# A four-layer graph network on one core: a larger dense part in the last layer, its own-weight products made a stage earlier, and wider sharing of overflow chunks

## The chip, the cores and the metric

The kernel runs on one core of a Trainium2 chip. The metric is the time of one execution in device microseconds, as the median over runs. The engines are named as in the profile: PE is TensorE (PEld its weight loads), DVE is VectorE, ACT is ScalarE, POOL is GpSimd, SP is SyncE, which issues most of the plain transfers.

## The reference

There are 6250 nodes with 256 features and 100000 edges (`src`, `dst`), sorted by `dst`. Four layers follow each other, each `x = layernorm(x + layer(x))` without gain:

```python
# layer 0: SAGE on h = relu(layernorm(x) * gamma + beta)
out = mean_over_edges(h[src] -> dst) @ W_l.T + b_l + h @ W_r.T
# layer 1: attention with 8 heads; softmax over the edges of one src
s = <q[src], k[dst]>; out = segment_sum(softmax(s) * v[dst], src) @ Wo + bo
# layer 2: two GAT passes with 4 heads, self loops, gelu; softmax over the edges of one dst
e = leaky_relu(alpha_s[src] + alpha_d[dst], 0.2); out = segment_sum(h[src] * softmax(e), dst) + b
# layer 3: SAGE, relu, a further product, residual, relu
mean = segment_sum(x[src], dst) / max(cnt, 1)
sage = mean @ W_l.T + b_l + x @ W_r.T
out = relu(relu(sage) @ W_ln.T + x)
```

## The kernel before

**Tiling.** The nodes are cut into `NB = 50` blocks of `B = 125`. The edges of a block are laid out in `CM = 16` chunks of 128 edges; what does not fit goes to `SH = 2` shared chunks, which one group of `GB = 10` blocks has in common (`NGR = 5` groups). A chunk's node rows are fetched from a table in HBM by an indirect transfer that POOL issues (`gather`, L927), 128 rows at a time, one instruction for each chunk. The sum over the edges of a block is then a product on PE: a one-hot matrix of the targets (made by DVE, or in layer 1 by PE and ACT) times the fetched rows.

**Stages.** The first stage, with its order of instructions written out by hand, normalises `x` in ten groups of five blocks (`Rows`) and stores them in three bf16 parts to `h_table` (`write`, L1170). Beside it, `by_target` makes the lists of edges by target, one part for each `next(lists)`. Then come five passes over the blocks: layer 0 (`piece0`, table `h_table`, with the lists by source made beside it in `by_source`), layer 1 (`piece1`, tables `kv_table` and `q_table`), the two GAT passes of layer 2 (`piece2`, `hs_tables`), and layer 3 (`piece3`, `x_table`). In layers 1 and 2 a pass has 200 pieces of four chunks.

**Order.** `run_pass` starts one piece after another and, at each start, advances every open piece by one `yield`, the oldest first; then it calls a function for work beside the pass. A scheduler may still move instructions on an engine. Gathers run ahead of their use by as many pieces as the `g` buffers hold: 7 in layer 1, 9 in layer 2, 5 in layer 3. The last step of a block is `finish0` to `finish3`. `finish2` of the second GAT pass updates `x_sb`, normalises it and stores its bf16 parts to `x_table`.

**The dense part of the last layer.** For the first `ND = 16` blocks of targets, layer 3 does not fetch edges. During the GAT passes, `count_edges` counts the edges from each source block to these targets: DVE compares target numbers with the edge ends (`a_hot`, L1897), PE multiplies (`a_acc`, L1919, one PSUM bank), ACT evicts a row group of `RB = 4` target blocks (500 columns) to `a_row` (L1906), and SP stores the row to `a_table` in bf16. Not all chunks can hold edges to a row group: `reach` gives the chunks for each. One step handles up to three chunks of one row group, and one step is made for each piece. In layer 3 `dense` loads rows of `x_table` (`xs`) and counts (`cnt`), 50 pairs of loads, and multiplies them (L2180); `RATE` spreads this over the first 80% of the pieces of the other 34 blocks. `finish3` makes the products with `W_l` and `W_r` (L923), the relu, the product with `W_ln` and the last normalisation.

`move` splits a transfer over more than 112 partitions into 112 and the rest:

```python
if B > HW_SPLIT:
    eng.dma_start(out=to[:HW_SPLIT], in_=of[:HW_SPLIT])
    eng.dma_start(out=to[HW_SPLIT:], in_=of[HW_SPLIT:])
```

Of the kernel before, what the change touches and what calls it, by code (L numbers as in the profile page):

```python
# [8 lines left out]
I32 = mybir.dt.int32  # L9
F16 = mybir.dt.float16  # L10
# [6 lines left out]
P = 128  # L17
# [638 lines left out]
def gnn_stack_kernel(ctx: ExitStack, tc: tile.TileContext, ins, out):  # L656
# [21 lines left out]
    GB = max(n for n in range(1, 11) if NB % n == 0)  # L678
# [33 lines left out]
    ND, RB = 16, 4  # L712
# [10 lines left out]
    DC = max(c1 for c0, c1 in reach)  # L723

# [15 lines left out]
    with ExitStack() as fast:  # L740
# [45 lines left out]
        a_table = dram.tile([N, ND * B], BF16, name="a_table_f")  # L786
# [51 lines left out]
        def block_rows(table, b, n=1):  # L838

            t = table[b * B : (b + n) * B, :]  # L840
            return t if n == 1 else t.rearrange("(n p) d -> p n d", p=B)
# [269 lines left out]
        class Rows:  # L1111
# [57 lines left out]
            def write(self):  # L1169
                nc.sync.dma_start(out=block_rows(h_table, self.b0, self.n), in_=self.hp)  # L1170
# [17 lines left out]
        with tc.tile_pool(name="fst", bufs=1) as pool, tc.tile_pool(name="fh", bufs=2) as work, tc.tile_pool(  # L1188
# [26 lines left out]
            for t in range(len(groups) + 5):  # L1215
                for r in group(t - 4):
                    r.low()
                for r in group(t - 3):
                    r.high()
                for r in group(t - 1):  # L1220
                    r.normal()
                if t == 1:
                    nc.vector.tensor_copy(gamma_p, gamma)
                for r in group(t - 2):
                    r.gain(gamma_p, beta)
                for r in group(t):
                    r.variance()
                if 1 <= t <= 6 or t == len(groups) - 1:
                    next(lists)
                for r in group(t - 3):  # L1230
                    last_h = r.rest()
                for r in group(t - 5):
                    r.write()
# [635 lines left out]
        beside_2 = ExitStack()  # L1869
        ap = beside_2.enter_context(tc.tile_pool(name="fa", bufs=2))  # L1870
        apsum = beside_2.enter_context(tc.tile_pool(name="fap", bufs=1, space=bass.MemoryType.PSUM))

        def count_edges():


            nodes = ap.tile([P, ND, B], F16, name="a_nodes", bufs=1)
            nc.vector.scalar_tensor_tensor(
                nodes, iota[:, :ND, None].to_broadcast([P, ND, B]), float(B),
                iota_p[:, None, :B].to_broadcast([P, ND, B]), op0=ALU.mult, op1=ALU.add,
# [10 lines left out]
            for k in range(len(steps) + 2):  # L1890
                if k < len(steps):
                    s, r, cs = steps[k]
                    if s not in sts:
                        sts[s] = one_hots(ap, key_s[:, s, :DC], DC, DC, 2, F16, "a_st")
                    hots[k] = ap.tile([P, 3, RW], F16, name="a_hot", bufs=3)
                    for i, c in enumerate(cs):
                        nc.vector.tensor_scalar(  # L1897
                            hots[k][:, i, :], nodes[:, r * RW : (r + 1) * RW], ends[:, s, c : c + 1], None,
                            op0=ALU.is_equal,
                        )  # L1900
                if k >= 2:
                    s, r, cs = steps[k - 2]
                    if cs[-1] == reach[r][1] - 1:
                        if r == 0:
                            rows[s] = ap.tile([B, ND * B], BF16, name="a_row")
# [24 lines left out]
        for layer in range(2):  # L1930
            table = hs_tables[layer]
            with tc.tile_pool(name=f"f2{layer}", bufs=1) as pool, tc.tile_pool(
# [4 lines left out]
                bias = load_row(pool, ins[f"L2_gnn_b{layer}"], "bias")  # L1937
                w_gat = gat_weight(pool, work, 1) if layer == 0 else None
                sums, held, shared, late = {}, {}, {}, []

                def finish2(b):
# [17 lines left out]
                    else:  # L1959
# [5 lines left out]
                        move(nc.sync, block_rows(x_table, b), xp.rearrange("p k d -> p (k d)"))  # L1965

# [90 lines left out]
                run_pass([(lambda a=a: piece2(*a)) for a in pieces((4, 4, 4, 4))], lambda t: next(counting, None))  # L2057
# [15 lines left out]
        beside_2.close()  # L2073
# [3 lines left out]
        with tc.tile_pool(name="f3", bufs=1) as pool, tc.tile_pool(name="f3w", bufs=2) as work, tc.tile_pool(  # L2077
# [5 lines left out]
            w_r = load_weight(pool, ins["L3_gnn_W_r"], "w_r")  # L2083
# [7 lines left out]
            def finish3(b, aT=None):  # L2091

                if aT is None:
                    agg = work.tile([B, D], F32, name="agg")
                    nc.scalar.activation(agg, sums.pop(b)[:B], AF.Copy, scale=rdeg[:, b, :])
                    yield
                    sum_T = kept(work, turned(bank(), agg), "aT")
                    yield
                xT = kept(work, turned(bank(), x_sb[:, b, :]), "xT")
# [3 lines left out]
                if aT is None:  # L2103
                    product(po, [(sum_T, w_l), (xT, w_r)])
                    nc.vector.tensor_add(s, po, b_l[:B, :])
                else:
                    product(po, [(aT, w_l)])
                    nc.vector.scalar_tensor_tensor(s, po, rdeg[:, b, :], b_l[:B, :], op0=ALU.mult, op1=ALU.add)
                    yield
                    po = bank()[:B, :D]  # L2110
                    product(po, [(xT, w_r)])
                    nc.vector.tensor_add(s, s, po)
# [44 lines left out]
            def load(k):  # L2157
# [3 lines left out]
                cnt = work.tile([B, 2, GW], BF16, name="cnt", bufs=LEAD + 2)  # L2161
                rows = a_table[s * B : (s + 2) * B, d * GW : (d + 1) * GW]
                move(nc.sync, cnt, rows.rearrange("(n p) d -> p n d", p=B))
                return xs, cnt

            ready = []

            def dense():
                loads = {k: load(k) for k in range(LEAD)}
                for k, (d, s) in enumerate(order):  # L2170
                    if k + LEAD < len(order):
                        loads[k + LEAD] = load(k + LEAD)
                    xs, cnt = loads.pop(k)
# [86 lines left out]
```

## Time and profile before

| | us |
|---|---|
| median of 14 runs (lowest, highest) | 5158.46 (5152.07, 5162.97) |
| the profiled execution: its own time | 5164.1 |
| its span, first to last instruction | 5162.3 |
| busy: PE, DVE, ACT, POOL | 4241.6, 3532.5, 2163.5, 3776.6 |
| start of the first and of the last gather from `h_table` | 149.2 to 1249.3 |
| start of the first and of the last gather from `kv_table` | 1235.4 to 2289.8 |
| start of the first and of the last gather from `hs_tables` | 2333.3 to 4421.4 |
| start of the first and of the last gather from `x_table` | 4443.3 to 5134.3 |

The profile is of one execution. A line of its list of groups has the source line, engine, operation, what is written and read, the count, the busy time and the mean of one in ns, and after the bar the idle time of the engine ahead of these instructions with what ended most of it. "issue" means that the engine waited for nothing that the profile shows. The rows by stage give the busy time of each engine within a stretch of the span. Matmuls are pipelined, so a mean duration of one is longer than what it adds to a row of them.

### The profile page before, as it was taken

The page shows a single profiled execution, that of the slowest core. Times are in us where ns is not written, and L with a number is a line of the kernel's source. Part 1 is how long each engine was busy: PE and PEld are TensorE (multiplying, and loading weights), DVE is VectorE, ACT ScalarE, POOL GpSimd, SP SyncE. Part 2 cuts the span into 40 slices and gives each one's busy share as a digit, 9 for nine tenths or more (in the row PEclk, how much of TensorE's full clock was granted, in tenths as well). Part 3 has the DMA queues.
Part 4 walks back from the last instruction along what each step waited for, and adds up shares of the span by engine and source line. Part 5 has one row for each costly group of instructions (what it writes and reads, how often), then busy time and mean ns, then how long its engine had stood idle before and what let it go on. Part 6 is the DMA issues. An engine that isn't in the chain of part 4 may idle for free. (4 is left out here: it accounts for less than half of the span.)

```text
span 5162.3 us, 84598 instructions
## 1 busy us (share of the span) xinstructions
PE 4241.6 (82%) x27926; PEld 3093.3 (60%) x27926; DVE 3532.5 (68%) x10485; ACT 2163.5 (42%) x6203; POOL 3776.6 (73%) x3889
## 2 busy tenths in 40 slices
PE   0467899987999999987887878877777777799996
PEld 0245667666676666665666666655556566466665
DVE  7576788766888888876666666657777777423334
ACT  4011898895344444433444444434444444211122
POOL 6677777776777777757777777767777777677775
PEclk9777999998999999998989999988989998899998
DMA  4556677666777777764444444444444444788875
GB/s 131 145 155 176 178 193 192 186 175 176 222 226 227 223 227 226 226 177 122 132 132 134 135 131 134 129 117 131 132 132 134 132 138 135 210 244 241 248 206 142
DMA packets 365012, 883.97 MB, mean 171 GB/s; under 512 B 83596, under 2 KB 181954, under 8 KB 364562
## 3 DMA queue, kind: packets, MB, share of 16 engines
q0 software_dynamic: 232032, 702.40, 49.4%
q1 hardware_dynamic: 132530, 176.06, 11.7%
q8 instruction: 222, 3.64, 0.3%
q14 instruction: 228, 1.87, 0.1%
HBM read 791.50 MB, written 86.63 MB: 170 GB/s over the span
## 5 line engine op out<-in xcount | busy, mean ns | idle before, releaser
L927 POOL DMA_INDIRECT g<-hs_table_f,idx_d x1600 | 1538.0, 961 | 487.5 <-issue 419.8
L927 POOL DMA_INDIRECT g<-h_table_f,idx_d x800 | 795.2, 994 | 296.5 <-issue 209.0
L2048 PE MATMUL ps<-msg,st 128*125 128x260 f32 x3200 | 892.3, 422 | 73.2 <-DVE msg L1982 50.4
L927 POOL DMA_INDIRECT g<-kv_table_f,idx_s x784 | 747.4, 953 | 250.2 <-issue 184.0
L995 PE MATMUL ps<-g,st 128*128 128x256 bf16 (+1 forms) x4032 | 639.7, 285 | 194.2 <-DMA g<-h_table_f,idx_d 95.3
L2048 PEld LDWEIGHTS ps<-msg,st 128*125 128x125 f32 x3200 | 632.4, 205 | 210.0 <-issue 50.6
L927 POOL DMA_INDIRECT g<-x_table_f,idx_d x544 | 516.2, 949 | 186.7 <-issue 156.2
L995 PEld LDWEIGHTS <-st 128*128 128x128 bf16 x4536 | 447.1, 101 | 287.9 <-issue 180.8
L1982 DVE TENSOR_TENSOR msg<-g,pp 128x1024 f32<-128x1024 f32 x400 | 485.0, 1213 | 21.8 <-ACT pp L1979 18.3
L1976 DVE TENSOR_TENSOR e<-g,pe 128x16 f32<-128x16 f32 x400 | 67.8, 169 | 582.4 <-DMA g<-hs_table_f,idx_d 423.1
L2015 PE MATMUL pe<-ad_parts,ts 125*128 125x4 bf16 x4800 | 178.0, 165 | 323.0 <-DVE e L1976 278.6
L936 DVE TENSOR_TENSOR st<-iota_p,key_d 128x500 f32<-128x500 f32 (+1 forms) x550 | 409.7, 745 | 44.2 <-PE ps L995 25.6
L2015 PEld LDWEIGHTS <-ts 125*128 125x128 bf16 x4800 | 177.6, 97 | 435.7 <-issue 335.4
L1846 PE MATMUL ps<-msg,st 128*125 128x264 f32 x1600 | 420.0, 400 | 2.4 <-DVE msg L1780 2.3
L1979 ACT ACTIVATE pp<-r 128x16 f32<-128x16 f32 (+1 forms) x410 | 76.7, 187 | 616.5 <-DVE r L1970 423.1
L948 ACT CAST ts<-tp 125x512 bf16<-125x512 f32 x400 | 230.6, 577 | 248.1 <-PE tp L946 245.1
L1522 ACT ACTIVATE oa<-o,blk 125x128 f16<-125x128 f16 x800 | 312.5, 391 | 36.8 <-PE acc L1529 25.5
L1829 DVE TENSOR_TENSOR prod<-g,qe 128x512 f32<-128x512 f32 x400 | 270.5, 682 | 80.9 <-PE qe L1826 47.1
L1826 PE MATMUL qe<-q,ts 125*128 125x256 bf16 x2400 | 320.3, 277 | 6.2 <-DMA q<-q_table_f 3.3
L1897 DVE TENSOR_SCALAR a_hot<-a_nodes,a_ends 128x500 f16<-128x500 f16 x950 | 321.4, 366 | 3.0 <-PE a_acc L1919 2.8
L1846 PEld LDWEIGHTS ps<-msg,st 128*125 128x125 f32 x1600 | 282.2, 188 | 63.1 <-ACT st_s L978 2.5
L1919 PE MATMUL a_acc<-a_hot,a_st 128*128 128x500 f16 x950 | 291.5, 399 | 31.8 <-ACT a_row L1906 22.1
(463 smaller groups left out, 8715.3 us busy)
## 6 DMA issues: line engine op xcount, KB each, us to landing
g<-hs_table_f,idx_d POOLq DMA_INDIRECT x1600
a_table_f<-a_row SPq DMA_DIRECT2D x50, 437.5 KB
cnt<-a_table_f SPq DMA_DIRECT2D x50, 437.5 KB
xs<-x_table_f SPq DMA_DIRECT2D x50, 336.0 KB
g<-h_table_f,idx_d POOLq DMA_INDIRECT x800
g<-kv_table_f,idx_s POOLq DMA_INDIRECT x784
hs_table_f<-hs SPq DMA_DIRECT2D x100, 115.5 KB
own<-hs_table_f SPq DMA_DIRECT2D x100, 115.5 KB
```

The source lines that it names most:

```text
L927: nc.gpsimd.indirect_dma_start(out=g, out_offset=None, in_=table, in_offset=bass.IndirectOffsetOnAxis(ap=idx, axis=0))
L936: nc.vector.tensor_tensor(st, iota_p[:, None, :w].to_broadcast([P, n, w]), key[:, :, None].to_broadcast([P, n, w]), op=ALU.is_equal,)
L995: nc.tensor.matmul(ps[:, :m], st[:, i, :], g[:, i, k * D : k * D + m], start=(c0 + i == 0 and k == 2), stop=(c0 + i == CH - 1 and k == 0),)
L1522: nc.scalar.activation(oa, o1, AF.Copy, scale=val_a[:, at])
L1826: nc.tensor.matmul(qe[:, i, :], ts[:, i0 + i, :], q[:, k * D : (k + 1) * D], start=(k == 0), stop=(k == 2))
L1829: nc.vector.tensor_mul(prod[:, i0 : i0 + m, :], g[:, i0 : i0 + m, :D], qe[:, :m, :])
L1846: nc.tensor.matmul(sums[b], hot, m[:, i * H1 : (i + 1) * H1, :].rearrange("p h c -> p (h c)"), start=(c == 0), stop=(c == CH - 1),)
L1897: nc.vector.tensor_scalar(hots[k][:, i, :], nodes[:, r * RW : (r + 1) * RW], ends[:, s, c : c + 1], None, op0=ALU.is_equal,)
L1919: nc.tensor.matmul(accs[s, r], sts[s][:, c, :], hot[:, i, :], start=(c == reach[r][0]), stop=(c == reach[r][1] - 1),)
L1982: nc.vector.tensor_mul(msg[:, : n * H2, :C2].rearrange("p (n h) c -> p n h c", h=H2), g[:, :n, :D].rearrange("p n (h c) -> p n h c", h=H2) ...
L2015: nc.tensor.matmul(pe[:, i, :], ts[:, i, :], ad_parts[:, b, k, :], start=(k == 0), stop=(k == 2))
L2048: nc.tensor.matmul(sums[b][:B, : D + H2], hot, m[:, i * H2 : (i + 1) * H2, :].rearrange("p h c -> p (h c)"), start=False, stop=(c == CH - 1),)
```

## The change

`GB` becomes the largest divisor of 50 up to 25 instead of up to 10, so 25 blocks share two chunks, in `NGR = 2` groups. `ND` becomes 24, in six row groups. `a_table` and `a_row` have one byte for each count; layer 3 loads the bytes into `few`, and ACT widens them to bf16 (`wide_counts`), one pair of blocks ahead. The counting steps (`COUNT_STEPS`, 650) are dealt out as 0.55 of them over the first GAT pass and 0.47 over the second, so one or two for each piece. `a_nodes` holds one row group, and the compare subtracts an offset instead of reading another slice. `finish2` of the second GAT pass also transposes the new `x_sb`, multiplies it with `W_r` and stores the product to the new `xr_table`; `finish3` loads it (`xr`), adds `b_l`, and then has one product with `W_l` only. In the first stage `write` goes through `move`, and one `next(lists)` stands at t = 11 instead of t = 9.

```diff
-    GB = max(n for n in range(1, 11) if NB % n == 0)
+    GB = max(n for n in range(1, 26) if NB % n == 0)
...
-    ND, RB = 16, 4
+    ND, RB = 24, 4
...
+    COUNT_STEPS = NB * sum(-(-(c1 - c0) // 3) for c0, c1 in reach)
...
-        a_table = dram.tile([N, ND * B], BF16, name="a_table_f")
+        a_table = dram.tile([N, ND * B], U8, name="a_table_f")
+        xr_table = dram.tile([N, D], F32, name="xr_table_f")
...
             def write(self):
-                nc.sync.dma_start(out=block_rows(h_table, self.b0, self.n), in_=self.hp)
+                move(nc.sync, block_rows(h_table, self.b0, self.n), self.hp)
...
-                if 1 <= t <= 6 or t == len(groups) - 1:
+                if 1 <= t <= 6:
                     next(lists)
                 for r in group(t - 3):
                     last_h = r.rest()
+                if t == len(groups) + 1:
+                    next(lists)
...
                         nc.vector.tensor_scalar(
-                            hots[k][:, i, :], nodes[:, r * RW : (r + 1) * RW], ends[:, s, c : c + 1], None,
-                            op0=ALU.is_equal,
+                            hots[k][:, i, :], nodes, ends[:, s, c : c + 1], float(-r * RW), op0=ALU.subtract,
+                            op1=ALU.is_equal,
                         )
...
+                        xT = kept(work, turned(whole, x_sb[:, b, :]), "xT")
+                        yield
+                        product(whole[:B, :D], [(xT, w_r)])
+                        xr = work.tile([B, D], F32, name="xr")
+                        nc.scalar.copy(xr, whole[:B, :D])
+                        move(nc.sync, block_rows(xr_table, b), xr)
...
-                run_pass([(lambda a=a: piece2(*a)) for a in pieces((4, 4, 4, 4))], lambda t: next(counting, None))
+                made = pieces((4, 4, 4, 4))
+                share = COUNT_STEPS * (0.55 if layer == 0 else 0.47) / len(made)
+                def beside_2(t):
+                    for _ in range(int(share * (t + 1)) - int(share * t)):
+                        next(counting, None)
+                run_pass([(lambda a=a: piece2(*a)) for a in made], beside_2)
...
             def finish3(b, aT=None):
+                xr = work.tile([B, D], F32, name="xr", bufs=3)
+                move(nc.sync, xr, block_rows(xr_table, b))
                 if aT is None:
...
+                    aT = kept(work, turned(bank(), agg), "aT")
+                    scale = 1.0
+                else:
+                    scale = rdeg[:, b, :]
+                nc.vector.tensor_add(xr, xr, b_l[:B, :])
                 yield
...
+                product(po, [(aT, w_l)])
+                nc.vector.scalar_tensor_tensor(s, po, scale, xr, op0=ALU.mult, op1=ALU.add)
...
+            def wide_counts(few):
+                cnt = work.tile([B, 2, GW], BF16, name="cnt", bufs=3)
+                nc.scalar.copy(cnt, few)
+                return cnt
             def dense():
                 loads = {k: load(k) for k in range(LEAD)}
+                nexts = [wide_counts(loads[0][1])]
                 for k, (d, s) in enumerate(order):
                     if k + LEAD < len(order):
                         loads[k + LEAD] = load(k + LEAD)
-                    xs, cnt = loads.pop(k)
+                    xs, cnt = loads.pop(k)[0], nexts.pop(0)
+                    if k + 1 < len(order):
+                        nexts.append(wide_counts(loads[k + 1][1]))
```

## The prediction

> **What bounds the kernel now.** I read the page first, its list of costliest groups above all, then the busy times by stage, then the waits in each stage. The sum is made against the profiled execution: span 5162.3 us, 5164.1 us with what lies around it, 5.6 us above the median of 5158.5. "No change" means within 0.2% (10.3 us), about what a measurement of this kernel can tell.
>
> ```profile
> L927 POOL DMA_INDIRECT g<-hs_table_f,idx_d x1600 | 1538.0, 961 | 487.5 <-issue 419.8
> L927 POOL DMA_INDIRECT g<-kv_table_f,idx_s x784 | 747.4, 953 | 250.2 <-issue 184.0
> L927 POOL DMA_INDIRECT g<-x_table_f,idx_d x544 | 516.2, 949 | 186.7 <-issue 156.2
> L1897 DVE TENSOR_SCALAR a_hot<-a_nodes,a_ends 128x500 f16<-128x500 f16 x950 | 321.4, 366 | 3.0 <-PE a_acc L1919 2.8
> L1919 PE MATMUL a_acc<-a_hot,a_st 128*128 128x500 f16 x950 | 291.5, 399 | 31.8 <-ACT a_row L1906 22.1
> ```
>
> A gather takes 0.95 us on POOL and 0.30 us of issue follow: 1.25 us, and 16 of them (one block) 20.0 us. In the time line the blocks of every layer start 20.0 to 20.6 us apart with no wait between: POOL sets the pace nearly everywhere. So a gather taken away is worth 1.25 us, as long as nothing else is late next. The columns below are us of stretch, then busy us of PE, PEld, DVE, ACT and POOL, the granted clock, DMA share and GB/s; the rows are the second layer, the third layer's two attention passes and the last layer:
>
> ```profile
> 1333.00:2291.00 958.00, 946.46 (x5602) 662.53 (x5602) 837.11 (x1735) 397.16 (x1129) 725.16 (x764) 1.00 0.77 226
> ...
> 2333.00:3360.00 1027.00, 825.74 (x5835) 643.73 (x5836) 660.59 (x1806) 423.22 (x1198) 777.97 (x817) 0.92 0.48 132
> 3383.00:4422.00 1039.00, 802.01 (x5516) 612.60 (x5517) 752.16 (x2420) 447.83 (x1145) 790.41 (x816) 0.90 0.48 133
> ...
> 4466.00:5115.00 649.00, 615.63 (x3753) 420.74 (x3752) 235.45 (x1163) 118.70 (x311) 491.24 (x518) 0.99 0.84 230
> ```
>
> The attention passes leave PE about 200 us each. The second layer (PE 98.8% busy) and the last (95%) leave it almost nothing, though POOL still keeps its pace there. That decides this prediction: the change takes work from POOL and gives PE more.
>
> **Shared chunks (GB 10 to 25).** By the instruction counts of the changed program, gathers of shared chunks fall in the first layer from 10 to 4 (and the word lists from 10 to 4), in the second from 20 to 8, in the attention passes from 40 to 16. At 1.25 us that is 15, 15 and 30 us. First layer: -14. Second layer: PE idles only 11.5 of 958 us, so at most that much of the 15 comes back: -9 (bounds -2 and -15).
>
> **Split stores.**
>
> ```profile
> 127.97 2.55 POOL L1167 TENSOR_TENSOR hp<-h,hp 125x1280 bf16<-125x1280 f32 x1 [2.67 <-ACT hp L1166]
> 149.25 1.05 POOL L927 DMA_INDIRECT g<-h_table_f,idx_d  x1 [18.73 <-DMA b_q<-in_L_gnn_bq]
> ```
>
> ```profile
> 132.00:149.00 17.00, 2.62 (x10) 2.07 (x10) 2.84 (x17) 0.98 (x2) 0.00 (x0) 1.00 0.58 177
> ```
>
> POOL has finished the rows at 130.5 us and waits 18.7 us. The releaser named is a weight load; but the ten stores of 939.9 KB go out from 52 us on, at a DMA share of 0.31 and 102 GB/s (window 50 to 100 us), so 9.6 MB end about where the gather starts. Split stores that run at the 177 GB/s of the row 132:149 leave only the last 1 MB to land, 5.4 us behind its issue at 131.6 us, and some 2 us until a reader sees it (L2140 started 1.95 us after the `x_table` store that it waits for was issued): 139 us, or -10. Moving the list step from t = 9 to 11 puts its 6 us of DVE and 4 us of ACT behind the ninth group, where DVE idled 2.7 and 4.1 us: up to 3 us against it, within the bounds 0 and -14. The Trainium skill, "DMA: Bandwidth & Descriptors", section "Why a DMA increments its semaphore by 16 and not by 1", says that a copy uses the largest number of engines up to 16 that divides its outer dimension: 5 for 125 partitions, which is the 0.31; its section "Rules for kernel authors" says that halving a transfer by partitions isn't worth it, which would give 0 here.
>
> **More counts in the attention passes.** Six row groups reach 33 chunks per block instead of 19: 700 more `a_hot` and 700 more matmuls. The new pace gives the first attention pass 0.55 of the steps, 907 instead of 475 (+432), the second the rest (+268). DVE: 432 x 0.366 = 158 us and 8 for wider `a_st`, 827 of the 1012 us that 12 fewer gathers leave (82%); in the second 752 + 98 + 7 = 857 of 1024 (84%). A second scalar operation costs nothing in the nearest rows: L1238 with two took 0.58 us on 800 four-byte values, L1027 with one 0.58. PE: 291.5/950 = 0.307 us each, 133 and 82 us. A boundary between row groups waits for the eviction of the one `a_acc` bank (L1906, 0.58 + 0.20 us); in the changed order on PE at most four matmuls stand between in 104 of 299 boundaries (before: 2 of 199), each leaving some 0.4 us open: 27 and 15 us. The own-weight products add, by the rows of the last layer, 53.6 us (L923 w_r) and 20 (transposes of `x_sb`) to the second attention pass. Sums: PE 826 + 133 + 27 = 986 of 1012 us, and 802 + 82 + 15 + 74 = 973 of 1024. Tight, but the second layer holds 1.25 us per gather at 98.8% PE and 87% DVE, and the clock there is 1.00 against 0.92 here.
>
> Between DVE and POOL: a gather took 954 ns (window 2400 to 3300), 970 in the second attention pass and 949 in the last, which has no `a_hot`. If all 5 ns come from 2.3 `a_hot` per piece, doubling them costs 800 x 5 = 4 us, and 4 more in the other layer. The same skill page, section "SWDGE vs HWDGE vs iDMA", says that GpSimd writes descriptors into SBUF that VectorE locks it out of in two-port modes; if every added `a_hot` held a gather up for its 366 ns, that would cost 256 us. No row here shows such a loss. Both layers: -30 + 8 = -22, with bounds -30 and, should PE lose 25 us more in each, +28.
>
> **The last layer.** 24 dense blocks leave 26 x 16 gathers and 4 shared ones: 132 fewer, 165 us off POOL, 692 to 527. But PE is full there. By busy time per instruction (window 4500 to 5100): 600 more dense matmuls at 0.224 are +134; 432 fewer gather matmuls at 0.132 are -57, 200 w_r halves at 0.260 -52, 116 transposes at 0.19 -22: PE has +3 us in all. In the chain of waits 12 dense matmuls take 2.54 us (0.212) while PE is full, and dense ends at 5000 us, 557 us behind the first gather:
>
> ```profile
> 4990.03 5.08 PE d L2180 x24
> ...
> 4997.51 2.55 PE d L2180 x12
> ```
>
> In the changed order the last dense matmul has in front of it 600 more dense matmuls (+127 us), but 342 fewer gather matmuls (-45), 112 fewer product halves (-29) and 74 fewer transposes (-14): +39, so dense ends 596 us behind the first gather. Until then POOL is held by its five buffers, at piece 66 of 78. The last 12 pieces take 6.67 us each on POOL, 80 us, and PE's rest at the same prices takes no longer (306 x 0.132 + 124 x 0.26 + 45 x 0.19 = 81); the end follows the last gather by 27 us as before: 596 + 80 + 27 = 703 against 719, -16. Bounds: -27 if PE closes its gaps, +25 if it waits. It can: the 75 widening copies of 2000 bytes on ACT, about 1.9 us each by L1166 (1.26 us for 1280), 143 us beside 119 busy, stand ahead of dense matmuls; a third of a microsecond lost on each is 25 us. The DVE add that waits for `xr` holds the one-hots queued behind it, covered by three `st` buffers and 36% DVE load. The last row of `xr_table` and the weight loads now stand ahead of the first loads on SP's queue: +2.
>
> **Sum.** -10 - 14 - 9 - 22 - 16 + 2 = -69: 5164 - 69 = 5095 for a profiled execution, 5089 for the median.
>
> **Rivals.** (1) Counting makes PE the bound of both attention passes. For: 97% and 95% by my sum, and 104 uncovered evictions. Against: busy sums overstate overlapped matmuls, and clock and second layer above. The other parts give -47, so the sign turns when a piece of these passes (400 in all) takes 0.12 us longer than now; at 0.3 us longer the total is -47 + 120 = +73, 5232, and with one pass hit -47 - 11 + 60 = +2, 5161. (2) The last layer stays POOL-bound and yields its whole 165 us: 5089 - 149 = 4940. Against: PE has some 660 us of work there (its busy time from 4422 us on) for 527. (3) The change does less than it says: the stores are not what POOL waits for and the second layer gives nothing, the last layer +25: -14 - 22 + 25 + 2 = -9, 5150.
>
> **Chances.** Forecast (5050 to 5130) 0.76; rival 1 0.10; rival 2 0.03; rival 3 and mixtures of bad ends 0.11, half of it within 0.2%. Range: the sum's favourable bounds give -14 - 15 - 15 - 30 - 27 = -101, 5057, to which I add a little for rival 2; upward rival 3's milder half. Faster 0.84, same 0.06, slower 0.10.
>
> **What would show it.** Right: first gather at 136 to 142 us; gathers still 1.25 us apart in the attention passes, PE over 90% there; POOL waiting for PE in the last layer, dense ending some 600 us into it, a last layer of about 700 us. Wrong: blocks of the attention passes over 20.8 us apart, `a_acc` waiting for `a_row` for more than 60 us in all, dense matmuls waiting for `cnt`, or the last layer under 660 us.

## The result, and the profile after

The changed kernel takes 5088.38 us (median of 6 runs, 5087.38 to 5093.28) against 5157.55 for the kernel before in the same comparison: a ratio of 0.9867, 95% interval 0.9857 to 0.9877. The forecast was 5089. The profiled execution took 5092.4 us, its span is 5090.6. Three of the later runs fell on a chip on which the kernel before itself took 6899 us, and nothing is concluded from them.

The total came out as forecast, but not from the places it was forecast from. The time between the first gathers from the tables, from the two traces, in us:

| kernel | to `h_table` | to `kv_table` | to `hs_tables` | to second pass | to `x_table` | to the end |
|---|---|---|---|---|---|---|
| before | 149.2 | 1086.2 | 1092.8 | 1055.0 | 1060.1 | 719.0 |
| after | 138.5 | 1069.9 | 1082.7 | 1038.6 | 1042.2 | 718.7 |
| difference | -10.7 | -16.3 | -10.1 | -16.4 | -17.9 | -0.3 |
| forecast | -10 | -14 | -9 | both passes: -22 | (see left) | -16 + 2 |

The columns are the first stage, the first layer, the second, the two attention passes and the last layer. The first attention pass is counted from its first shared gather, the second from its first gather by chunk, which comes 5.0 us later in both kernels. The differences add up to the -71.7 us between the spans; between the medians it is -69.2, since each profile is of one execution. How much of such a number is chance, the second layer tells: in the runs below that do not differ there from the changed kernel it took 1079.3 to 1087.7 us.

The rows by stage of the kernel after answer to those shown of before (us of stretch, then busy us of PE, PEld, DVE, ACT and POOL, granted clock, DMA share, GB/s): second layer, two attention passes, last layer.

```profile
1310.00:2251.00 941.00, 935.27 (x5559) 659.92 (x5559) 833.01 (x1711) 394.12 (x1115) 712.23 (x752) 1.00 0.77 226
2296.00:3320.00 1024.00, 872.83 (x6294) 660.24 (x6294) 792.16 (x2248) 466.95 (x1331) 767.04 (x804) 0.98 0.48 130
3337.00:4353.00 1016.00, 860.10 (x6046) 645.45 (x6043) 819.06 (x2652) 502.10 (x1294) 772.93 (x798) 0.96 0.50 136
4390.00:5045.00 655.00, 635.99 (x3639) 389.89 (x3639) 213.16 (x1044) 232.91 (x323) 372.27 (x392) 0.99 0.78 208
```

In the attention passes PE is at 85%, not at the 95 to 97% of my sum, and the clock went up from 0.92 and 0.90 to 0.98 and 0.96. In the last layer PE is at 97%, and POOL has fallen from 491 busy us of 649 to 372 of 655. What became of POOL's gain there is in the list of costliest groups:

```profile
L931 POOL DMA_INDIRECT g<-hs_table_f,idx_d x1600 | 1538.1, 961 | 487.4 <-issue 420.7
L1903 DVE TENSOR_SCALAR a_hot<-a_nodes,a_ends 128x500 f16<-128x500 f16 x1650 | 525.5, 366 | 5.3 <-PE a_acc L1925 5.1
L1925 PE MATMUL a_acc<-a_hot,a_st 128*128 128x500 f16 x1650 | 473.0, 385 | 92.3 <-ACT a_row L1912 74.9
L931 POOL DMA_INDIRECT g<-x_table_f,idx_d x416 | 396.3, 953 | 308.9 <-PE ps L999 167.0
```

128 gathers and four shared ones fewer are 165 us off POOL; POOL now waits 167.0 us for PE to give `g` buffers back. The exchange is complete: the last layer is as long as before (718.7 us for 719.0). The 1600 gathers of the attention passes have the same mean, 961 ns, with 700 more compares beside them. The one wait that I had named as a sign of failure, `a_acc` for `a_row`, did grow, from 22.1 to 74.9 us.

The first gather, in POOL's time line:

```profile
138.54 1.79 POOL L931 DMA_INDIRECT g<-h_table_f,idx_d  x1 [6.40 <-DMA h_table_f<-hp]
```

It started at 149.25 before, after 18.73 us of waiting that the profile put down to the load of a bias, `b_q` (the prediction calls it a weight load). Now the wait is 6.40 us, and its releaser is the store itself.

### The profile page after: what moved, and what is told of

It reads as the page before. It is cut to its first block, busy times and chain, and to the rows that moved or that the text cites. A ratio compares the mean times of both kernels' runs of the same rounds, so it can differ in the third digit from the quotient of the medians.

```text
span 5090.6 us, 87518 instructions
## 1 busy us (share of the span) xinstructions
PE 4348.9 (85%) x28778; PEld 3103.6 (61%) x28778; DVE 3713.0 (73%) x11039; ACT 2380.1 (47%) x6498; POOL 3601.7 (71%) x3709
## 4 chain that ended last, share of the span: by engine, by line
PE 41%; POOL 21%; issue 14%; DVE 12%; DMA 9%; ACT 2%; SPq 0%; DVEq 0%; ACTq 0%; POOLq 0%
POOL g L931 20%; PE ps L1852 8%; PE d L2205 7%; PE qe L1832 5%; DMA g<-hs_table_f,idx_d 5%; PE ps L999 4%; PE pt L927 3%; PE po L927 3%; PE acc L1535 3%; DVE a_hot L1903 3%; DVE msg L1996 2%; DMA g<-h_table_f,idx_d 2%; DVE st L940 1%; PE tp L978 1%; PE ps L2062 1%
## 5 line engine op out<-in xcount | busy, mean ns | idle before, releaser
L931 POOL DMA_INDIRECT g<-hs_table_f,idx_d x1600 | 1538.1, 961 | 487.4 <-issue 420.7
L2062 PE MATMUL ps<-msg,st 128*125 128x260 f32 x3200 | 845.7, 398 | 35.5 <-DVE msg L1996 21.4
L2062 PEld LDWEIGHTS ps<-msg,st 128*125 128x125 f32 x3200 | 602.0, 194 | 180.4 <-DVE msg L1996 20.4
L999 PE MATMUL ps<-g,st 128*128 128x256 bf16 (+1 forms) x3648 | 581.4, 285 | 143.4 <-DMA g<-h_table_f,idx_d 96.8
L931 POOL DMA_INDIRECT g<-x_table_f,idx_d x416 | 396.3, 953 | 308.9 <-PE ps L999 167.0
L1925 PE MATMUL a_acc<-a_hot,a_st 128*128 128x500 f16 x1650 | 473.0, 385 | 92.3 <-ACT a_row L1912 74.9
L999 PEld LDWEIGHTS <-st 128*128 128x128 bf16 x4104 | 403.7, 101 | 228.8 <-issue 142.1
L1903 DVE TENSOR_SCALAR a_hot<-a_nodes,a_ends 128x500 f16<-128x500 f16 x1650 | 525.5, 366 | 5.3 <-PE a_acc L1925 5.1
L2205 PE MATMUL d<-cnt,xs 125*128 125x500 bf16 x1800 | 393.1, 374 | 0.0
L1852 PEld LDWEIGHTS ps<-msg,st 128*125 128x125 f32 x1600 | 284.0, 188 | 61.1 <-ACT st_s L982 2.5
```

The lines of the kernel that those rows point to most:

```text
L931: nc.gpsimd.indirect_dma_start(out=g, out_offset=None, in_=table, in_offset=bass.IndirectOffsetOnAxis(ap=idx, axis=0))
L999: nc.tensor.matmul(ps[:, :m], st[:, i, :], g[:, i, k * D : k * D + m], start=(c0 + i == 0 and k == 2), stop=(c0 + i == CH - 1 and k == 0),)
L1852: nc.tensor.matmul(sums[b], hot, m[:, i * H1 : (i + 1) * H1, :].rearrange("p h c -> p (h c)"), start=(c == 0), stop=(c == CH - 1),)
L1903: nc.vector.tensor_scalar(hots[k][:, i, :], nodes, ends[:, s, c : c + 1], float(-r * RW), op0=ALU.subtract, op1=ALU.is_equal,)
L1925: nc.tensor.matmul(accs[s, r], sts[s][:, c, :], hot[:, i, :], start=(c == reach[r][0]), stop=(c == reach[r][1] - 1),)
L2062: nc.tensor.matmul(sums[b][:B, : D + H2], hot, m[:, i * H2 : (i + 1) * H2, :].rearrange("p h c -> p (h c)"), start=False, stop=(c == CH - 1),)
```

## The experiments

Theory: POOL's 1.25 us per gather sets the pace everywhere but in the last layer, where PE, full until the dense part ends, takes back all that POOL saves. So sharing and split stores make the whole gain, and the 24 dense blocks nothing. Rivals: the dense blocks do bring something and sharing less; the attention passes are close to being bound by PE or DVE; the last layer is held by transfers. The traces give for each run the same stages as above:

| kernel | first stage | first layer | second | attention 1 | attention 2 | last layer |
|---|---|---|---|---|---|---|
| before + sharing by 25 | 147.9 | 1068.3 | 1087.9 | 1034.9 | 1041.8 | 715.8 |
| before + split stores | 135.2 | 1086.9 | 1093.2 | 1055.9 | 1059.7 | 717.5 |
| after, 16 dense blocks | 139.3 | 1068.9 | 1083.1 | 1037.7 | 1039.6 | 717.5 |
| after, dense over 90% | 139.5 | 1068.8 | 1086.3 | 1038.8 | 1039.7 | 702.6 |
| after, own-weight products moved back | 139.4 | 1066.0 | 1079.3 | 1038.5 | 1039.2 | 741.8 |
| after, two-byte counts | 138.4 | 1065.9 | 1083.2 | 1038.3 | 1041.5 | 731.7 |
| after, list step at t = 9 | 136.4 | 1067.2 | 1087.7 | 1039.1 | 1044.0 | 716.1 |
| after, ten chunks for each row group | 138.7 | 1070.5 | 1083.3 | 1045.6 | 1043.8 | 715.9 |
| combined | 137.5 | 1063.5 | 1080.4 | 1034.9 | 1037.7 | 693.9 |

**Sharing alone, on the kernel before.**

```diff
-    GB = max(n for n in range(1, 11) if NB % n == 0)
+    GB = max(n for n in range(1, 26) if NB % n == 0)
```

> The kernel before with one edit: 25 blocks share two chunks instead of 10 (GB 25, NGR 2). Everything else is as before: 16 dense blocks with two-byte counts, the stores unsplit, the own-weight products in the last layer. My theory (POOL's 1.25 us per gather sets the pace of every layer while PE has room): 12 fewer gathers in each of the first and second layer's tables and 24 fewer in the two attention passes give -13, -13 (as measured between before and after) and -30; the last layer loses 8 to 10 of its 544 gathers less anything PE keeps back, 0 to -5. In all -55 to -60, so 5098 to 5103 us against 5158, a ratio of 0.989. Rival (the attention passes gained through their new counting order or something else in the change, not through the gathers): -25 to -30 only, 5130. If this alone gives as much as the whole change, the other parts add up to the split stores' 11 us and nothing else.

Measured: 5099.51 us, ratio 0.9888 (0.9871 to 0.9904), against 5159.31 before: -60, of the whole change's -69. Layer by layer it is about what the whole change gives: -18 in the first layer, -20 and -18 in the passes, but -5 instead of -10 in the second layer, which differs by 8 us among the runs that do not touch it. So, within some 4 us, nothing else in the change helped or hurt the attention passes, though it put 700 compares, 700 matmuls and the own-weight products into them.

**Split stores alone, on the kernel before.**

```diff
-                nc.sync.dma_start(out=block_rows(h_table, self.b0, self.n), in_=self.hp)
+                move(nc.sync, block_rows(h_table, self.b0, self.n), self.hp)
```

> The kernel before with one edit: the first stage's stores to h_table go out in two pieces, 112 rows and the rest; the list step stays at t = 9. Theory (the unsplit stores are late, and POOL's first gather waits for them): the first gather starts at 138 to 140 us instead of 149.2, the total falls by 10 to 11, 5147 us, a ratio of 0.998; the wait named at the first gather falls from 18.7 to 6 to 8 us. Rival A (the releaser named, the weight load, is the real one): first gather stays at 149, total 5158. Rival B (the list step at t = 9 is what held the stores' rows up, so that the move of the step was needed too): first gather at 142 to 146, total 5151 to 5155.

Measured: 5148.77 us, ratio 0.9975 (0.9965 to 0.9984), -10.5. POOL's time line of this run:

```profile
126.32 2.54 POOL L1167 TENSOR_TENSOR hp<-h,hp 125x1280 bf16<-125x1280 f32 x1 [2.67 <-ACT hp L1166]
135.17 1.89 POOL L927 DMA_INDIRECT g<-h_table_f,idx_d  x1 [6.30 <-DMA h_table_f<-hp]
```

The bias load named before was not the cause: its instruction is untouched, and the wait fell from 18.73 to 6.30 us. The records of the transfers settle it. The ten stores are 6250 packets of 1540 bytes; the last of them ends at 147.7 us in the kernel before, at 134.0 in this run and at 137.4 in the changed kernel, and the first gather starts 1.2 to 1.5 us behind that in all three. Unsplit, these packets never move at more than 123 GB/s in any microsecond; split, at up to 333. The rows are even done 1.7 us earlier than before (128.9 against 130.5), so the late list step is not needed for this gain. Together the two edits, -60 and -10.5, are the whole change's gain of 69; for its largest part, the dense blocks with all that serves them, nothing is left over that the intervals, 5 to 9 us to either side, would show.

**16 dense blocks in the changed kernel.**

```diff
-    ND, RB = 24, 4
+    ND, RB = 16, 4
```

> The changed kernel with 16 dense blocks instead of 24; the one-byte counts, the own-weight products in the second attention pass, the sharing by 25 blocks and the split stores all stay. It gives POOL back 128 gathers in the last layer (160 us) and takes 600 dense matmuls off PE there, and 700 compares and 700 matmuls out of the attention passes. Theory A (with 24 dense blocks PE is the bound of the last layer, and what POOL saved went into its waits for PE): the last layer is POOL-bound again, about 34 x 16 gathers at 1.25 us plus a tail of 26, some 705 to 715 us against 718.7; the total is 5075 to 5090 us, the same as or a little under the changed kernel's 5088. The attention passes stay as they are, since the compares are beside the gathers. Theory B (the 24 dense blocks are what gains in the last layer, and moving the products saves little): the last layer is 735 or longer, the total over 5105.

Measured: 5087.47 us, ratio 0.9860 (0.9844 to 0.9877), the same as with 24; the last layer takes 717.5 instead of 718.7. But the bound is the other one. POOL's waits in the last layer of this run:

```profile
POOL g L931 <- issue: 150.2, 493, 0.3
POOL g L931 <- DMA g<-x_table_f,idx_d: 8.2, 27, 0.3
POOL g L931 <- PE d L2205: 2.7, 9, 0.3
```

```profile
4390.00:5040.00 650.00, 586.13 (x3492) 384.80 (x3491) 248.50 (x1204) 190.04 (x312) 492.15 (x519) 0.96 0.83 223
```

No wait is longer than 0.3 us: POOL goes at its own pace, 548 gathers at 1.25 us, 685 us (686.3 by the trace), and PE idles 64 of 650 us. With 24 blocks it is PE's turn. The two sizes lie on either side of a balance, and cost the same.

**The dense part spread over 90% of the pieces.**

```diff
-            RATE = ND // (2 * RB) * NB / (0.8 * len(made))
+            RATE = ND // (2 * RB) * NB / (0.9 * len(made))
```

> The changed kernel with the dense matmuls of the last layer spread over the first 90% of its pieces instead of the first 80%; the same work. Theory A (PE is full while dense matmuls go on, and the last pieces afterwards go at POOL's pace with PE partly idle: 85 us from the end of dense to the last gather): a later, thinner spread lets gathers start earlier, dense ends at 620 to 640 us behind the first gather, and the last layer takes 690 to 705 us instead of 718.7; total 5062 to 5075. Theory B (PE's own sum of work, 636 busy of 655 us, bounds the whole layer, wherever the dense matmuls stand): within 5 us of the changed kernel, 5083 to 5093. Theory C (too late a spread leaves dense blocks' last steps behind the last gather): slower, 5095 or more.

Measured: 5071.74 us, ratio 0.9828 (0.9808 to 0.9848); the last layer takes 702.6 us. The dense part ends 631 us behind the first gather instead of 607, the last gather comes 654 behind it instead of 690, and POOL's waits for PE are 127.3 instead of 167.0 us:

```profile
POOL g L931 <- PE ps L999: 127.3, 42, 5.7
```

PE's work is the same; with the thinner spread, gathers run while PE is full, and less than 30 us of gathers is left for the time after it. The end now follows the last gather by 48 us instead of 29: the last eight dense blocks become ready together and pass through their last steps two at a time.

**Own-weight products back in the last layer.**

```diff
-                        product(whole[:B, :D], [(xT, w_r)])
...
-                product(po, [(aT, w_l)])
+                if aT is None:
+                    product(po, [(sum_T, w_l), (xT, w_r)])
```

> The changed kernel with the products with W_r, and the transposes before them, back in the last layer's last steps; no xr_table. Everything else of the change stays (24 dense blocks, one-byte counts, sharing by 25 blocks, split stores). Theory A (PE's sum of work bounds the last layer with 24 dense blocks): PE gets 50 x 4 product halves at 0.215 us and 100 transposes at 0.15 to 0.19 us more there, 43 + 15 to 19 = 58 to 62 us, so the last layer takes 770 to 785 us instead of 718.7, and the second attention pass stays at 1042 since POOL sets its pace: total 5140 to 5155. So the move is what made 24 dense blocks cost nothing against 16. Theory B (POOL, with its five buffers, or the transfers of counts and rows hold the last layer, and PE's gaps take up the products): within 10 us of the changed kernel, 5085 to 5098. Theory C (the move cost the second attention pass something): that pass falls below 1035.

Measured: 5112.31 us, ratio 0.9915 (0.9898 to 0.9931), +24; last layer 741.8, +23; second attention pass 1039.2 for 1042.2, inside the spread of the runs that do not differ there (1039.2 to 1044.0). The direction is theory A's, the size is not. The row of the last layer, and the only wait of PE that the profile names there (4390 to 5055 us):

```profile
4380.00:5055.00 675.00, 672.99 (x3846) 422.28 (x3845) 206.18 (x969) 240.51 (x355) 367.75 (x387) 1.00 0.71 189
```

```profile
PE pt L913 <- ACT s L2126: 0.8, 2, 0.6
```

PE idles 2 us of 675, where in the changed kernel it idled 19 of 655. So 17 us of the added work went into gaps. The rival that transfers hold the last layer falls here: with `xr` gone the DMA share fell from 0.78 to 0.71, and the layer became longer. The added work is smaller than I put it, too: by the time line of the kernel after, four product halves take 0.86 us (4722.06 to 4722.92) and two transposes 0.22, so 200 halves and 100 transposes are 43 + 11 = 54 us:

```profile
4722.06 1.03 PE L927 MATMUL pt<-w_ln,sT 128*125 128x256 f32 x4
4722.92 0.38 PE L914 MATMUL pt<-ident,agg 125*128 125x125 f32 x2
4723.14 2.13 PE L999 MATMUL ps<-g,st 128*128 128x256 bf16 x18
4725.10 5.25 PE L2205 MATMUL d<-cnt,xs 125*128 125x500 bf16 x24
4730.19 1.03 PE L927 MATMUL pt<-w_l,aT 128*125 128x256 f32 x4
```

And 60 of the halves and 30 of the transposes stand behind the end of the dense part, where they cost nothing: the dense part ends 633.9 us behind the first gather, 27 later than in the changed kernel, but from there to the end of the kernel it is 107.9 us here and 111.8 there. The move of these products is what pays for the change from 16 to 24 blocks: with it both take the same (717.5 and 718.7), and without it the layer with 24 takes 741.8.

**Two-byte counts, and no widening.**

```diff
-                        a_table = dram.tile([N, ND * B], U8, name="a_table_f")
+                        a_table = dram.tile([N, ND * B], BF16, name="a_table_f")
...
-                nc.scalar.copy(cnt, few)
-                return cnt
+                return few
```

> The changed kernel with counts stored and loaded as bf16 and no widening copies on ACT in the last layer; a_table has twice the bytes. Theory A (PE's work bounds the layer; ACT's 75 widening copies are hidden and transfers have room): last layer 712 to 722 us, total 5082 to 5092. Theory B (dense matmuls wait for ACT's copies, as my bound of +25 us feared): last layer 695 to 705, total 5065 to 5075. Theory C (the doubled bytes make the loads late; DMA share 0.78 in this stage): last layer over 725.

Measured: 5099.92 us, ratio 0.9894 (0.9877 to 0.9910), +11; last layer 731.7, +13. Theory A fell, theory C holds. The edit takes the copies away and doubles the bytes at once, so +13 is what the bytes cost less what the copies cost. That the copies, which I had priced at up to +25, cost little is seen in the changed kernel itself, where no wait of a dense matmul for `cnt` is named. In the last layer's row the DMA share goes from 0.78 to 0.90 and PE idles 28 of 655 us:

```profile
4390.00:5045.00 655.00, 627.33 (x3581) 382.70 (x3579) 204.59 (x1011) 95.40 (x240) 360.05 (x379) 0.99 0.90 231
```

DVE's wait for `xr` there, first of the kernel after, then of this one:

```profile
DVE xr L2124 <- DMA xr<-xr_table_f: 101.3, 35, 16.0
```

```profile
DVE xr L2124 <- DMA xr<-xr_table_f: 180.3, 39, 22.1
```

The load of `xr` stands on SP's queue behind the loads of counts and rows, and SP itself is now held up with those two named as releasers (`few` 50.4 us, `xs` 37.0, against 17.9 and 18.1 in the changed kernel). That the 13 us come by way of `xr` is the likeliest reading; a run with `xr` on another queue was not made.

**The list step back at t = 9.**

```diff
-                if 1 <= t <= 6:
+                if 1 <= t <= 6 or t == len(groups) - 1:
                     next(lists)
```

(and the call at t = 11 removed)

> The changed kernel with the list step back at t = 9 in the first stage. By the run with the split stores alone, whose first gather started at 135.2 us against 138.5 in the changed kernel: the step's place costs 3 us, so the first gather starts at 135 to 136, and the total falls by 3. Rival (the 25-block lists, not the place, make the difference): first gather at 138 to 140.

Measured: one time, 5092.3 us. The first gather starts at 136.4 us, 2.1 before the changed kernel's. The other traces with split stores agree: with the step at t = 11 the first gather starts at 138.4 to 139.5 us in seven of them, with the step at t = 9 at 135.2 to 137.5 in five. So the place costs some 2 us of the 3 that the prediction allowed; the spans, 5090.5 and 5090.6, do not show it.

**Ten chunks for each row group: a load test.**

```diff
-        reach.append((c0, min(CM, int(place_of((g1 + 1) * GQ * EQ, 1)) // P + 1)))
+        reach.append((0, 10))
```

> The changed kernel with all six row groups of the counting compared against ten chunks of every source block, 3000 compares and matmuls instead of 1650; the added ones find nothing. A load test of the attention passes: +743 and +607 of each. Theory A (passes at POOL's pace as long as DVE and PE have room, and the busiest engine's sum when they have not): DVE would have 792 + 743 x 0.366 = 1064 us in the first pass and 819 + 222 = 1041 in the second, PE 873 + 743 x 0.26 = 1066 and 860 + 158 = 1018, against 1038.6 and 1042.2 us taken now: 1070 to 1100 and 1045 to 1070, total 5125 to 5175. Theory B (each compare on DVE holds a gather on POOL up): gathers from hs_tables longer than 1.0 us on the mean, and +300 us or more. Theory C (PE's modelled busy time overstates, and DVE's compares run under other waits, so there is more room than the sums say): within 15 us of the changed kernel.

Measured: 5099.99 us (only two times, both this one), ratio 0.9890 (0.9870 to 0.9910). 1350 compares and matmuls more cost 7.0 us in the first pass and 1.6 in the second: theory C.

```profile
2296.00:3320.00 1024.00, 997.74 (x7011) 720.52 (x7011) 990.08 (x2979) 479.50 (x1324) 774.33 (x806) 1.00 0.48 130
3337.00:4353.00 1016.00, 936.79 (x6574) 676.25 (x6573) 994.16 (x3236) 494.47 (x1288) 772.24 (x801) 0.99 0.50 137
```

```profile
L931 POOL DMA_INDIRECT g<-hs_table_f,idx_d x1600 | 1541.0, 963 | 487.5 <-issue 388.8
L1925 PE MATMUL a_acc<-a_hot,a_st 128*128 128x500 f16 x3000 | 794.2, 375 | 37.5 <-ACT a_row L1912 16.9
```

DVE is at 97 and 98% and PE at 97 and 92%, and the pass still goes nearly at POOL's pace. The mean gather went from 961 to 963 ns. The wait of `a_acc` for `a_row`, 74.9 us in the changed kernel, is down to 16.9. The likely reason, not tested by itself, is that with more matmuls per row group there is more to put between two evictions.

**Two parts of the dense rows; and all blocks sharing two chunks.** These three belong to the 6899.23 us of the kernel before.

```diff
-                        for j in (2, 1, 0):
+                        for j in (1, 0):
```

> The changed kernel with the dense matmuls of the last layer made for two of the three bf16 parts of x_table's rows (1200 matmuls instead of 1800; the smallest part is left out of the sums of the dense blocks). All transfers, copies and gathers stay. Theory A (PE holds the last layer until the dense part ends): PE loses 600 x 0.212 = 127 us, POOL's waits for PE (167 us) shrink to 50 or less, the last gather comes 565 to 585 us behind the first instead of 690 (420 gathers at 1.25 are 525), and the layer takes 595 to 620 us instead of 718.7: total 4965 to 4990. Theory B (the transfers of counts, rows and gathers, at a DMA share of 0.78, or the five buffers of gathered rows hold it): the layer falls by less than 40 us, total over 5048.

```diff
-    GB = max(n for n in range(1, 26) if NB % n == 0)
+    GB = max(n for n in range(1, NB + 1) if NB % n == 0)
...
-            RATE = ND // (2 * RB) * NB / (0.8 * len(made))
+            RATE = ND // (2 * RB) * NB / (0.87 * len(made))
```

> The changed kernel with all 50 blocks sharing the two chunks (GB 50, NGR 1), the dense matmuls spread over the first 87% of the pieces, and the list step back at t = 9. Theory: two more sharing groups saved are worth 4 gathers in each of the first two layers, 4 in each attention pass: -5, -1 to -5 (PE is full in the second layer), -10, and 2 behind PE's work in the last layer: 0; the later spread gives the last layer -12 to -18, the list step 0 to -2. Total -28 to -38 from the changed kernel's 5088, 5050 to 5060. Rival (shared chunks are not the price: the steps from 5 groups to 2 gained by what runs beside them): -12 to -18 only, 5070 to 5076.

```diff
+            RATE = ND // (2 * RB) * NB / (0.9 * len(made))
...
-                if ready and len(late) < 2:
+                if ready and len(late) < 3:
```

> As the run with 87%, but spread over the first 90%, and with up to three finished dense blocks in their last steps at once instead of two. In the run with 90% alone the last gather came 654 us behind the first, and the end 48 us behind that, since the last dense blocks followed each other. Theory (the tail is a chain of steps of the dense blocks, which three at once shorten): last gather at 652 to 656, end 30 to 38 us behind it, the last layer 684 to 694 us; total 5040 to 5052. Rival (the tail is DVE's or PE's work): end still 48 us behind, the layer 702, total 5055 to 5065.

Measured: 6743.76, 6774.86 and 6766.04 us, ratios to that 6899.23 of 0.9774, 0.9813 and 0.9797. On that chip, layers that no edit touched took 36 to 42% longer than elsewhere (the attention passes of the first of the three 1412 and 1436 us), with the gathers themselves as short as ever (953 ns on the mean) and 1214.2 us of waits between those of the two passes instead of 487.4. The expectations are made for another pace; these runs decide nothing, and how the last layer behaves with a third of the dense work gone was not seen in comparable runs.

**Combined.** The kernel of the last of these three again, beside a kernel before of 5160.05 us.

> All 50 blocks share the two chunks (GB 50, NGR 1), the dense matmuls go over the first 90% of the pieces with up to three finished dense blocks in their last steps at once, and the list step is back at t = 9. By the price of a gather in undisturbed runs (1.25 us): first layer -5, second -1 to -5, attention passes -5 each, so 1033 to 1036 and 1034 to 1037 us for them. Last layer: by the run with 90% alone 702.6 (last gather 654 behind the first, end 48 behind that); three blocks at once shorten the end to 30 to 38, 684 to 694. Total 5040 to 5052. Rival (the end is DVE's work, not a chain): end still 48 behind, the layer 702, total 5055 to 5062. Rival on sharing (what the passes gained by 25 was not the gathers): passes as before, total 5060 or more.

Measured: 5044.03 us (5040.74 to 5049.81), ratio 0.9775 (0.9762 to 0.9789). It beats both kernels, as the theory said. The two attention passes take 1034.9 and 1037.7 us, 3.7 and 4.5 less than the changed kernel's, where four gathers fewer in each are 5. The last layer is 693.9: last gather 651 behind the first, end 43 behind that, so with three blocks at once the end is 5 us shorter than in the run with 90% alone, and not 10 to 18 as expected; each of the two numbers is of one execution.

## Why the prediction came true, point by point

That the total came within 1 us was luck: two misses cancelled. The last layer gave nothing (-0.3) where -14 was forecast (-16, and +2 for SP's queue), and the attention passes gave 34 where 22 was. Of the signs named, the first gather, the pace of the gathers and POOL's wait for PE came as forecast; PE over 90% in the attention passes (85%) and a last layer of about 700 us (718.7) did not.

**Pace and shared chunks: right.** As the price of a gather taken away, 1.25 us holds where POOL sets the pace. Twelve fewer in an attention pass are 15 us, and from the first to the last gather by chunk the passes went from 1025.3 to 1010.7 and from 1038.1 to 1022.4 us: -14.6 and -15.7. Twelve fewer in the first layer are 15, and it gave 16.3; four fewer in each pass of the combined kernel are 5, and they gave 3.7 and 4.5. The second layer gave about 10 with PE at 99% of its stretch; its spread from run to run, 8 us, is nearly as large.

**Split stores: right**, by the reason given (the stores end where the gather starts) and against the releaser that the profile named. Rival 3 falls with it: the stores alone move the first gather by 14 us (10.5 by the medians, since the profiled execution before lies 5.6 above its median). The rule of the Trainium skill ("DMA: Bandwidth & Descriptors", section "Rules for kernel authors") against halving a transfer by partitions would have given 0; for 125 partitions cut into 112 and 13 the runs show -10.5, and the measurement decides.

**Attention passes: the terms that I added were not there.** The +8 for DVE and POOL getting in each other's way, read out of a difference of 5 ns between windows, is nil: 961 ns on the mean with 950 compares and with 1650, 963 with 3000. The other 4 us lie at the ends of the passes: from the last gather by chunk of the first pass to the first of the second 22.9 us instead of 24.6, and from the last of the second to the first from `x_table` 19.8 instead of 22.0. What shortened them was not tested; the run with the sharing alone has them as well (22.7 and 19.3). The lock that the same page of the skill describes in its section "SWDGE vs HWDGE vs iDMA" shows in none of these runs; whether these compares run in the two-port mode that it needs, no run tells.

PE's 986 and 973 us were wrong the other way. I added new work at 0.307 us a matmul to a busy time measured at a clock of 0.92. The mean duration in PE's largest group of both passes goes with the clock; before, after and in the load test it is:

```profile
L2048 PE MATMUL ps<-msg,st 128*125 128x260 f32 x3200 | 892.3, 422 | 73.2 <-DVE msg L1982 50.4
L2062 PE MATMUL ps<-msg,st 128*125 128x260 f32 x3200 | 845.7, 398 | 35.5 <-DVE msg L1996 21.4
L2062 PE MATMUL ps<-msg,st 128*125 128x260 f32 x3200 | 839.5, 388 | 38.6 <-DVE msg L1996 25.8
```

At clocks of 0.91, 0.97 and 0.995 (the mean of the two passes), 422, 398 and 388 ns times clock are 384, 386 and 386. The small `pe` matmuls do not follow, 165 ns in all three, so what comes now is an estimate. At the clock of after, the old 825.74 us are 825.74 x 0.92 / 0.98 = 775, and the 432 matmuls added 98, which is about 0.23 each; in the load test, 717 more in the same window added 997.74 x 1.00 - 872.83 x 0.98 = 142, or about 0.20 each, near the 0.212 of a dense matmul in a full row. Rival 1 had been kept at 0.10 on the strength of these sums; the load test shows that twice as much again would hardly have woken it. "`a_acc` waits for `a_row` for more than 60 us" was a bad sign to choose: it came true, in a PE with 150 us to spare in each pass.

**The last layer: mechanism right, size missed.** PE decides until the dense part ends and POOL after it, as forecast. Of the 15.7 us that 718.7 lies above 703, 10.9 are the end of the dense part (606.9 for 596), 3.3 the tail up to the last gather (83.3 for 80), 1.6 the rest (28.6 for 27). Within the 10.9, the first dense matmul came 21.5 us behind the first gather instead of 16.6: I had moved that start along unchanged, though the loads ahead of it had changed. With 16 dense blocks and the rest of the change it is 21.4, with two-byte counts 19.1, with the own-weight products back 18.1; which load it is was not tested. The remaining 6 are the prices. What leaves PE's row was priced by busy time per instruction: gather matmuls 0.132, product halves 0.260, transposes 0.19, together 88 us. Start to start, in a full row (the time line above), they are 0.109, 0.215 and 0.11: 342, 112 and 74 of them give 37 + 24 + 8 = 69 us. What was added, dense matmuls at 0.212, had been priced start to start. The gaps on PE that closed (33 us idle of 649 before, 19 of 655 after) hid the rest of that error. The feared wait for the widening copies did not come; the bytes that they save, less what the copies cost, are worth some 13 us, a gain that my sum had not named at all.

## What to carry to other kernels

Moving work from the engine that sets the pace to one that is full buys nothing beyond the balance point: look first at how the work is spread within the stage (one constant, 0.8 to 0.9, gave 16 us of the last layer here, where 128 gathers fewer gave none). Price matmuls start to start from a full row of the time line, for what is removed as for what is added, and, where the granted clock differs, put busy times on one clock before comparing or adding: without that the 432 added matmuls would seem to cost 0.11 us each (872.83 less 825.74), with it 0.23, and a full row has 0.212. To know how much room an engine has, load it: the sums said 97% with 907 counting matmuls in the first attention pass, and with 1680 of them by the trace the pass took only 7 us more.

## What was not expected of the hardware

In the attention passes the granted TensorE clock was higher where PE had more to do: 0.92 and 0.90 with PE busy 80 and 77% before, 0.98 and 0.96 at 85%, 1.00 and 0.99 at 97 and 92% in the load test. The busy share alone does not tell the clock, since the first layer of the kernel after has 0.89 at 85% (805 of 950 us). And 3000 compares on VectorE in place of 950 lengthened the mean indirect gather on GpSimd by 2 ns.
